# A new order for the same instructions: S and A blocks of several batches side by side on TensorE

## Chip, cores and metric

The kernel runs on one core of one Trainium2 chip. The time is the device time of one launch in microseconds (us); the median of several runs counts, and one more execution was taken by the hardware profiler.

## What is computed

The input x has 128 batches of 128 tokens (rows) by 512 features. adj is a 128 by 128 matrix, about one eighth of it not zero. Two layers follow each other, each with a residual and a normalization. Cut to what matters:

```
# layer 0: a product with adj, its maximum over the 512 columns, relu
C   = einsum('od,bdn->bon', adj, x) + b          # A is the same without b, so only
out = max over the last axis of relu(A_j + (C - A)_i)   # a row maximum of adj @ x is needed
x   = layernorm(x + out)

# layer 1: masked attention with 8 heads of 64, then a projection
q, k, v = split(x @ w_qkv)                       # 512 -> 3 x 512
attn = softmax(where(adj == 0, -inf, q @ k.T / 8))
o    = (attn @ v) @ w_proj + b_proj
x    = layernorm(x + o + layernorm(o) * gamma + beta)
```

## The kernel before

The 128 batches are worked in 32 groups of four. Within a group g, the batches b = 4g + i carry the index i = 0 to 3. All five queues (TensorE, VectorE, ScalarE, GpSimd and SP, which issues nearly all DMAs) are in an order written out by hand: no engine picks its next instruction by itself.

**How the order is made.** A step is a small function, such as S(b) or rest(g, j). Each step has a place, a number in planned microseconds from the group's start. Group g's places are moved by g times PERIOD, all places of all groups are sorted, and the steps are emitted in that order. So a place has no effect on the chip but through the order that comes out of it:

```
u0 = g * PERIOD
...
b, u = g * G + i, u0 + u
...
plan.sort(key=lambda p: p[:2])
with tc.manual_schedule(engines={E.PE, E.Activation, E.DVE, E.Pool, E.SP}):
    for _, _, f, a in plan:
        f(*a)
```

There are tables for groups 0 and 1 (FIRST), for the last two (LAST), for all the others (STEADY), and one for the weights and constants (SETUP). TWO says which steps use a two-bank tile or GpSimd. Waits between engines follow from the emitted order: a step that touches a tile waits for the steps ahead of it, in that order, that touch the same tile.

**The steps on TensorE.** All results lie in PSUM, where there are four one-bank buffers (ps_1) and two two-bank buffers (ps_2).

- conv(b), line 486: adj times x of one batch, for layer 0. Two matmul instructions.
- dm(g, j) and dd(g, j), lines 670, 671 and 676: the dense products for q, k and v. Operands are split into a high part h, a low part l and a difference d, so that one product is eight matmuls (dm: h times h, l times l) and four more (dd: d times d), into two banks. j = 0 to 3 are v of the four batches; j = 4 to 11 are column blocks of q and k, each for all four batches at once. Columns j = 0, 4 and 6 take one ps_2 buffer for both banks; the others take two ps_1 buffers.
- S(b), line 716: the scores q times k of one batch, 16 matmul instructions with 64 rows of the array, into a ps_2 buffer.
- AV(b), line 802, called A below: attention times v, 16 matmul instructions with 64 columns of the array.
- po(b) and pod(b): the projection, in the same eight and four matmuls as dm and dd; of the four batches, i = 2 takes a ps_2 buffer.

**The steps around them.** load(b) brings x in; cmax reduces conv's result on VectorE; relu, rstdx, shiftx and others on GpSimd make row factors, norm0 on ScalarE applies them. xpl, xrow and xcross transpose x through DRAM: ScalarE splits each word into two planes, SP writes them out and reads them back with a transposing DMA. xmask and xsub (VectorE), xhigh (ScalarE, or GpSimd for i = 0) and xd (VectorE or GpSimd) make the h, l and d parts of x, in buffers x_forms that there are once, with a slice for each batch of a group. So xhigh(b) of one group may write its slice only when the dense products of the group before have read it. main (ScalarE) takes the first bank of a dense product out, rest (VectorE) adds the second.

After S come masked and rmax (VectorE), exps (ScalarE, 16 instructions), recip and wts (VectorE), then pln (ScalarE), row and cross (SP), the same way through DRAM: cross(b), line 780, delivers the transposed weights eT that A(b) reads. After A come omask and osub (VectorE), ohigh (ScalarE or GpSimd), od (VectorE or GpSimd), then po and pod, pmain and prest (VectorE, they free the banks), sq1, st1, n1a, n1b, sq2, st2, norm2 for the last normalizations, with n1a and n1b (lines 892 and 865) on VectorE, and reso, resx, resb (the residual) and the small row operations on GpSimd. out(b) stores the result.

Of the kernel before, what the change touches and what calls it, by code (L numbers as in the profile page):

```python
# [26 lines left out]
PERIOD = 54.43882  # L27
STEADY = {
    'load': [-90.979, -98.210, -86.366, -88.446],
    'conv': [-75.080, -64.352, -67.023, -70.602],  # L30
    'cmax': [-72.886, -63.292, -64.469, -65.979],
    'relu': [-62.380, None, -61.262],
    'bn': [-85.283, -78.072],
    'ba': [-76.773, -76.871],
    'rstdx': [-64.783],
    'shiftx': [-61.992],
    'add0': [None, None, -60.500, -55.763],
    'sq0': [None, None, -56.469, -54.924],
    'rstd0': [None, None, -54.874],
    'shift0': [None, None, -23.855],  # L40
    'norm0': [-59.794, -61.212, -52.725, -52.013],
    'xpl': [-58.956, -54.218, -49.889, -44.844],
    'xrow': [-57.883, -53.145, -48.816, -43.301],
    'xcross': [-54.573, -50.568, -46.622, -40.435],
    'xmask': [-47.658, -42.468, -38.679, -34.118],
    'xsub': [-43.076, -38.349, -34.726, -32.646],
    'xhigh': [-47.158, -38.788, -33.148, -33.668],
    'xd': [-37.151, -28.807, -25.122, -23.029],
    'dm': [3.754, 7.444, 16.569, 13.785, -22.455, -31.523, -27.895, -19.783, -26.082, -24.268, -29.709, -4.527],
    'dd': [9.258, 19.289, 20.196, 11.065, -13.491, -8.148, -10.819, -9.055, -17.969, -15.305, -11.726, -2.714],  # L50
    'main': [9.110, 14.458, 21.811, 16.171, -10.671, -29.055, -11.156, -17.770, -24.069, -22.256, -17.285, -2.515],
    'rest': [12.301, 26.117, 23.001, 18.511, -5.215, -4.627, -1.871, -7.670, -15.367, -8.258, -10.618, -1.282],
    'S': [0.000, 0.970, 6.474, 15.599],
    'masked': [1.171, 4.033, 8.388, 26.711],
    'rmax': [2.907, 10.127, 14.634, 29.080],
    'exps': [6.022, 11.370, 22.296, 32.668],
    'recip': [11.253, 17.788, 27.842, 35.882],
    'wts': [12.895, 20.651, 37.253, 41.757],
    'pln': [16.656, 25.869, 38.513, 45.479],
    'row': [20.902, 29.660, 40.435, 47.401],  # L60
    'cross': [24.543, 33.020, 43.404, 51.435],
    'AV': [37.376, 47.198, 53.539, 64.603],
    'omask': [39.660, 48.620, 56.741, 72.345],
    'osub': [40.380, 50.401, 60.612, 73.544],
    'ohigh': [44.959, 51.471, 59.941, 73.606],
    'od': [48.023, 56.076, 68.476, 77.554],
    'po': [48.098, 56.379, 66.410, 75.542],
    'pod': [52.632, 60.006, 72.821, 94.480],
    'pmain': [51.968, 62.227, 76.840, 84.645],
    'prest': [53.745, 63.958, 78.638, 95.588],  # L70
    'res': [39.182, 60.502, 66.017, 83.629],
    'resx': [49.373, 64.496, 76.714, 86.509],
    'resb': [50.221, 68.714, 78.821, 88.081],
    'reso': [57.343, 70.378, 81.767, 96.358],
    'sq1': [57.577, 74.126, 82.111, 96.308],
    'sm1': [59.687, 67.486, 83.015, 100.647],
    'st1': [58.591, 75.013, 87.275, 102.706],
    'n1a': [59.947, 79.246, 91.027, 101.796],
    'n1b': [61.551, 82.391, 92.834, 105.448],
    'sq2': [64.986, 90.195, 98.692, 112.722],  # L80
    'sm2': [65.262, 89.331, 93.678, 113.836],
    'st2': [65.873, 91.082, 99.579, 114.416],
    'norm2': [72.898, 97.014, 105.313, 123.821],
    'out': [73.732, 100.113, 108.144, 131.860],
# [3 lines left out]
        'load': [-339.216, -336.022, -299.318, -292.716],  # L88
        'conv': [-320.211, -319.706, -263.923, -261.033],
        'cmax': [-287.550, -269.059, -253.277, -242.604],  # L90
        'relu': [-265.160, -255.522, -248.695, -239.422],
        'bn': [-289.729, -282.267, -262.447, -251.751],
        'ba': [-286.976, -275.167, -254.963, -248.112],
        'rstdx': [-273.222, -264.798, -251.699, -242.168],
        'shiftx': [-255.673, -255.423, -248.481, -238.547],
        'norm0': [-247.810, -241.423, -241.293, -231.100],
        'tx': [-239.998, -240.970, -235.970, -229.175],
        'copy': [-231.539, -232.867],
        'pv': [-186.452, -231.512],
        'keep': [-144.699, -223.445],  # L100
        'xmask': [-227.206, -233.390, -231.343, -223.813],
        'xsub': [-226.502, -230.254, -230.249, -179.216],
        'xhigh': [-210.161, -227.313, -226.698, -211.953],
        'xd': [-159.790, -216.301, -207.483, -146.722],
        'dm': [None, None, 14.000, 16.573, -19.708, -43.109, -33.492, -6.250, -23.281, -14.646, -35.590, -6.060],
        'dd': [None, None, 21.026, 20.229, -8.181, 0.474, -26.083, -12.473, -20.232, -14.110, -31.477, -1.951],
        'main': [None, None, 19.638, 24.293, -7.213, -26.572, -17.941, -3.776, -17.267, -10.053, -30.978, -2.703],
        'rest': [None, None, 21.313, 28.301, -4.316, 2.523, -15.800, 0.777, -7.778, -4.529, -14.235, 1.449],
        'S': [3.939, 4.174, 12.958, 20.307],
        'masked': [7.850, 9.636, 14.415, 22.403],  # L110
        'rmax': [8.329, 12.699, 21.343, 22.643],
        'exps': [13.089, 15.014, 24.976, 29.418],
        'recip': [16.256, 21.430, 34.750, 34.644],
        'wts': [20.131, 32.286, 38.995, 35.803],
        'pln': [22.222, 35.478, 41.768, 50.996],
        'row': [25.064, 45.158, 49.252, 57.729],
        'cross': [30.795, 46.513, 49.735, 59.800],
        'AV': [37.520, 47.772, 52.279, 66.968],
        'omask': [39.391, 49.259, 54.469, 70.965],
        'osub': [40.545, 53.566, 61.562, 72.912],  # L120
        'ohigh': [41.247, 52.725, 63.738, 71.968],
        'od': [50.703, 55.119, 66.836, 79.701],
        'po': [48.210, 53.595, 72.824, 76.960],
        'pod': [53.374, 57.260, 74.590, 81.809],
        'pmain': [51.767, 58.323, 83.163, 78.361],
        'prest': [54.212, 62.992, 84.049, 83.271],
        'res': [-6.851, 71.276, 49.227, 88.351],
        'resx': [22.755, 76.004, 61.128, 89.325],
        'resb': [32.496, 77.502, 65.105, 93.272],
        'reso': [55.887, 77.786, 86.372, 95.300],  # L130
        'sq1': [57.019, 72.242, 87.119, 86.554],
        'sm1': [57.798, 71.222, 86.212, 89.323],
        'st1': [67.763, 73.225, 87.146, 93.420],
        'n1a': [59.485, 81.416, 88.540, 103.102],
        'n1b': [69.341, 86.827, 89.211, 103.699],
        'sq2': [71.896, 89.208, 97.526, 112.672],
        'sm2': [75.269, 87.809, 90.158, 110.923],
        'st2': [75.788, 90.664, 99.514, 118.898],
        'norm2': [80.561, 97.480, 99.819, 134.926],
        'out': [82.775, 109.802, 103.140, 135.391],  # L140
    },
    {
        'load': [-144.852, -133.466, -152.643, -139.868],
        'conv': [-135.661, -121.160, -124.230, -125.568],
        'cmax': [-114.732, -91.366, -100.617, -106.235],
        'relu': [-83.301, None, -88.339],
        'bn': [-123.347, -101.036],
        'ba': [-122.535, -99.486],
        'rstdx': [-86.661],
        'shiftx': [-83.240],  # L150
        'add0': [None, None, -65.496, -86.773],
        'sq0': [None, None, -61.309, -81.741],
        'rstd0': [None, None, -59.490],
        'shift0': [None, None, 5.293],
        'norm0': [-74.823, -65.297, -57.477, -48.421],
        'xpl': [-69.704, -59.513, -56.889, -44.324],
        'xrow': [-60.039, -58.141, -47.326, -41.960],
        'xcross': [-60.034, -44.291, -41.474, -40.784],
        'xmask': [-51.323, -42.090, -40.930, -39.239],
        'xsub': [-44.906, -41.006, -36.993, -36.881],  # L160
        'xhigh': [-38.422, -39.691, -36.673, -37.554],
# [5 lines left out]
        'S': [-1.994, -0.002, -0.960, 21.339],  # L167
        'masked': [-0.617, 5.427, 2.141, 24.207],
        'rmax': [1.990, 8.305, 12.703, 26.036],
        'exps': [5.200, 16.787, 23.670, 28.218],  # L170
        'recip': [8.307, 19.928, 31.918, 29.464],
        'wts': [16.401, 28.492, 33.827, 37.853],
        'pln': [18.886, 28.689, 39.281, 43.942],
# [834 lines left out]
```

## Time and profile before

| What | Value |
|---|---|
| median of three runs | 1896.47 us (1894.26 to 1897.58) |
| the profiled execution | 1887.61 us, its span 1885.8 us |
| busy: TensorE, VectorE, ScalarE, GpSimd | 98%, 85%, 82%, 74% of the span |
| granted TensorE clock | 0.997 of full speed |
| DMA | 302.92 MB, mean 161 GB/s |
| issue to landing, median: cross, xcross, load | 4.3, 3.3, 3.0 us |
| first S at | 49.0 us |
| first S of the last group at | 1816.9 us |

The span runs from the first to the last instruction of the core; the execution's time lies around it. Busy time counts the profiled durations of instructions. For TensorE these overlap from one matmul to the next, so a step is better read as the difference of two starts. In profile lines, PE is TensorE, PEld its weight loads, DVE VectorE, ACT ScalarE and POOL GpSimd. "x16" at the end is the number of merged instructions, and in square brackets stands idle time ahead of a line and what ended it.

### The profile page before, as it was taken

The numbers are of one execution on the slowest core, as the hardware profiler recorded it, in microseconds if no ns is written. First come the engines' busy times: TensorE is split into PE (matmuls) and PEld (weight loads), VectorE is DVE, ScalarE is ACT, GpSimd is POOL, SyncE is SP. The second block draws the span as 40 slices with busy tenths as digits, with TensorE's granted clock in tenths as the row PEclk, the third lists the DMA queues.
The fourth block names the chain that finished last, engine by engine and source line by source line (L and its number), as shares of the span: only waits on it lengthen the run. The fifth ranks groups of instructions, "written<-read, shape, count | busy, mean of one in ns | idle before, by whom it ended". The sixth has DMA issues, their size and how long they took to land. (4 is left out here: it accounts for less than half of the span.)

```text
span 1885.8 us, 32740 instructions
## 1 busy us (share of the span) xinstructions
PE 1842.2 (98%) x10541; PEld 1417.9 (75%) x10541; DVE 1597.0 (85%) x2584; ACT 1542.4 (82%) x3927; POOL 1387.2 (74%) x1935
## 2 busy tenths in 40 slices
PE   8999999999999999999999999999999999999995
PEld 5677777777777777777777777777777777777774
DVE  7989888889888889888898888898888988888887
ACT  6977888888888888888888788888888888888775
POOL 4266787787777787777787777877777877777768
PEclk9999999999999999999999999999999999999998
DMA  5666566566565665665665656656566656666451
GB/s 149 158 159 169 162 169 164 166 161 176 154 173 160 161 184 163 156 164 166 160 186 147 164 163 166 178 162 160 160 168 167 180 147 169 168 163 171 141 139 51
DMA packets 486140, 302.92 MB, mean 161 GB/s; under 512 B 399440, under 2 KB 403664, under 8 KB 485968
## 3 DMA queue, kind: packets, MB, share of 16 engines
q1 hardware_dynamic: 485104, 299.70, 58.8%
q8 instruction: 84, 1.38, 0.3%
q10 hardware_dynamic: 864, 1.12, 0.2%
q14 instruction: 88, 0.72, 0.1%
HBM read 72.16 MB, written 131.07 MB: 108 GB/s over the span
## 5 line engine op out<-in xcount | busy, mean ns | idle before, releaser
L755 ACT ACTIVATE e<-e,nmax 128x128 f32<-128x128 f32 x1016 | 392.4, 390 | 0.0
L862 POOL TENSOR_TENSOR xb<-xb,o 128x512 f32<-128x512 f32 x125 | 199.5, 1596 | 77.1 <-DVE o L865 74.7
L770 ACT COPY planes<-e 128x2048 uint16<-128x2048 uint16 x124 | 234.8, 1893 | 20.6 <-DVE e L764 18.7
L876 POOL TENSOR_SCALAR sum<-sum 128x1 f32<-128x1 f32 (+1 forms) x287 | 99.1, 345 | 207.1 <-ACT square L871 193.2
L871 ACT ACTIVATE square<-o,sum 128x512 bf16<-128x512 f32 x256 | 183.4, 716 | 75.1 <-DVE o L865 74.2
L877 POOL TENSOR_TENSOR sum<-sum,mhalf 128x1 f32<-128x1 f32 (+1 forms) x287 | 212.8, 742 | 23.9
L755 ACT ACTIVATION_READ_ACCUMULATOR e<-e,nmax 128x1 f32 x1016 | 192.8, 190 | 0.0
L730 DVE SCALAR_TENSOR_TENSOR e<-psc,mask 128x1024 f32<-128x1024 f32 x127 | 154.3, 1216 | 42.5 <-PE psc L716 42.2
L858 POOL TENSOR_TENSOR xb<-xb,beta_sb 128x512 f32<-128x512 f32 x128 | 180.4, 1409 | 2.8
L764 DVE TENSOR_TENSOR e<-e,sums 128x1024 f32<-128x1024 f32 x128 | 159.5, 1246 | 0.0
L738 DVE TENSOR_REDUCE nmax<-e 128x8 f32<-128x1024 f32 x127 | 153.4, 1208 | 0.2
L607 POOL TENSOR_TENSOR x_d<-x_h,x_l 128x512 fp32r<-128x512 f32 x97 | 141.1, 1456 | 11.3 <-DVE x_l L613 10.2
L802 PEld LDWEIGHTS pav<-eT,v 128*64 128x64 f32 x2048 | 109.2, 136 | 49.1 <-issue 22.8
L716 PEld LDWEIGHTS psc<-qkT 64*128 64x128 f32 x2048 | 121.9, 187 | 31.1 <-issue 17.0
L802 PE MATMUL pav<-eT,v 128*64 128x128 f32 x2048 | 140.1, 279 | 3.2 <-DVE v L699 2.6
L716 PE MATMUL psc<-qkT 64*128 64x128 f32 x2048 | 140.7, 282 | 1.8 <-DVE qkT L699 1.4
L575 ACT COPY xplanes<-xt 128x1024 uint16<-128x1024 uint16 x124 | 128.7, 1038 | 15.8 <-DMA rowsx<-xplanes 14.6
L761 DVE RECIPROCAL sums<-sums 128x8 f32<-128x8 f32 x128 | 24.6, 192 | 133.1 <-ACT e L755 133.1
L486 PE MATMUL pa<-xt,adjT 128*128 128x512 f32 x256 | 134.7, 613 | 0.4 <-DVE adjT L415 0.4
L558 ACT ACTIVATE xt<-xt,sum 128x512 f32<-128x512 f32 x128 | 101.1, 810 | 40.4 <-POOL sum L552 20.4
L855 POOL TENSOR_SCALAR xb<-xb,sum 128x512 f32<-128x512 f32 x128 | 100.7, 787 | 34.5 <-DMA xb<-in_x_dram 33.2
L865 DVE SCALAR_TENSOR_TENSOR o<-o,sum,xb 128x512 f32<-128x512 f32 x128 | 125.3, 979 | 0.6
(4665 smaller groups left out, 5689.3 us busy)
## 6 DMA issues: line engine op xcount, KB each, us to landing
rows<-planes SPq DMA_DIRECT2D x124, 512.0 KB, 3.3
xt<-in_x_dram SPq DMA_DIRECT2D x128, 256.0 KB, 3.0
xb<-in_x_dram SPq DMA_DIRECT2D x128, 256.0 KB, 2.9
out_dram<-o SPq DMA_DIRECT2D x128, 256.0 KB, 3.0
rowsx<-xplanes SPq DMA_DIRECT2D x124, 256.0 KB, 2.8
wraw<-in_L_gnn_w_qkv_dram SPq DMA_DIRECT2D x8, 256.0 KB, 2.9
xT<-rowsx SPq DMA_TRANSPOSE x124, 3.3
eT<-rows SPq DMA_TRANSPOSE x124, 4.3
```

The source lines that it names most:

```text
L607: engine.tensor_tensor(d, h.bitcast(FP), l.bitcast(FP), op=ALU.subtract)
L716: nc.tensor.matmul(psc[:, s, hp, :], qkT[hs, hp, i, :], qkT[hs, KC + hp, i, :], start=not with_mask, stop=not with_mask or hp == HP - 1,)
L730: nc.vector.scalar_tensor_tensor(es[b], pscs.pop(b).rearrange("p s a m -> p (s a) m"), scale, mask_b, op0=ALU.mult, op1=ALU.add,)
L738: nc.vector.tensor_reduce(nmaxs[b], es[b], AX.X, ALU.max, negate=True)
L755: nc.scalar.activation(es[b][:, j, :], src[:, j, :], AF.Exp, bias=nmax[:, j : j + 1], scale=by, accum_out=sums[b][:, j : j + 1],)
L764: nc.vector.tensor_tensor(es[b], es[b], sums.pop(b)[:, :, None].to_broadcast([P, H, P]), op=ALU.mult,)
L770: nc.scalar.copy(pl, es.pop(b).rearrange("p h m -> p (h m)").bitcast(U16).rearrange("p (m s) -> p s m", s=2),)
L802: nc.tensor.matmul(pavs[b][s * HD : (s + 1) * HD, hp, :], v[:, h * HD : (h + 1) * HD], eT[:, s * HP + hp, :], start=True, stop=True,)
L858: nc.gpsimd.tensor_tensor(xbs[b], xbs[b], beta_sb, op=ALU.add)
L862: engine.tensor_tensor(xbs[b], xbs[b], os[b], op=ALU.add)
L871: nc.scalar.activation(square, src, AF.Square, bias=s[:, 0:1], scale=-float(D), accum_out=s[:, 1:2],)
L877: nc.gpsimd.tensor_tensor(s, s, mhalf[:, :n], op=ALU.pow)
```

## The change

No function is changed, and no instruction is added or removed; TWO is as it was. Changed are the numbers: PERIOD and all places in STEADY, FIRST, LAST and SETUP. The lines of STEADY that the text below speaks of (column i or j from left to right):

```diff
-PERIOD = 54.43882
+PERIOD = 55.65721
...
-    'xrow': [-57.883, -53.145, -48.816, -43.301],
-    'xsub': [-43.076, -38.349, -34.726, -32.646],
...
-    'dm': [3.754, 7.444, 16.569, 13.785, -22.455, -31.523, -27.895, -19.783, -26.082, -24.268, -29.709, -4.527],
-    'dd': [9.258, 19.289, 20.196, 11.065, -13.491, -8.148, -10.819, -9.055, -17.969, -15.305, -11.726, -2.714],
-    'main': [9.110, 14.458, 21.811, 16.171, -10.671, -29.055, -11.156, -17.770, -24.069, -22.256, -17.285, -2.515],
...
-    'S': [0.000, 0.970, 6.474, 15.599],
-    'cross': [24.543, 33.020, 43.404, 51.435],
-    'AV': [37.376, 47.198, 53.539, 64.603],
-    'ohigh': [44.959, 51.471, 59.941, 73.606],
-    'po': [48.098, 56.379, 66.410, 75.542],
-    'pod': [52.632, 60.006, 72.821, 94.480],
-    'prest': [53.745, 63.958, 78.638, 95.588],
...
+    'xrow': [-64.641, -56.635, -53.368, -45.398],
+    'xsub': [-48.801, -42.437, -37.819, -35.400],
...
+    'dm': [4.837, 11.201, 6.655, 16.122, -27.595, -10.169, -22.140, -32.141, -33.960, -23.959, -25.777, -30.323],
+    'dd': [9.383, 10.292, 20.788, 27.152, -12.896, -6.532, -8.350, -5.623, -4.714, -16.490, -7.441, -11.987],
+    'main': [7.711, 13.218, 9.668, 20.862, -11.380, -7.877, -11.865, -20.987, -31.942, -21.472, -23.760, -26.046],
...
+    'S': [0.000, 0.997, 13.110, 14.107],
+    'cross': [24.197, 29.995, 47.113, 59.806],
+    'AV': [37.158, 54.685, 53.762, 70.756],
+    'ohigh': [46.552, 56.528, 63.853, 84.748],
+    'po': [51.853, 58.675, 73.718, 96.599],
+    'pod': [57.646, 64.130, 75.536, 100.236],
+    'prest': [61.894, 65.455, 82.210, 102.843],
```

A place below zero is brought into a period by adding PERIOD: after, dd(g, 4) stands at -12.896 + 55.657 = 42.761 of the period ahead of its group. Sorted, TensorE's order over one period is as follows. A digit is i or j; a prime is the group before, a plus the group after; conv is that of the group after next.

```
before: S0 S1 po1' dm0 pod1' S2 dm1 dd0 A3' dd3 po2' dm3 S3 dm2 pod2' dd1 dd2 po3'
        dm5+ dm10+ dm6+ dm8+ dm9+ dm4+ conv0 dm7+ dd8+ A0 conv3 dd9+ pod3' dd4+
        conv2 dd10+ dd6+ conv1 dd7+ dd5+ A1 po0 dm11+ dd11+ pod0 A2
after:  S0 S1 pod0' po1' dm0 dm2 pod1' dd0 dd1 dm1 S2 S3 A3' dm3 po2' pod2' dd2
        dm8+ dm7+ dm11+ dd3 dm4+ dm10+ dm9+ dm6+ conv1 conv0 A0 conv3 dd9+ conv2
        po3' dd4+ dd11+ pod3' dm5+ dd6+ dd10+ dd5+ dd7+ dd8+ po0 A2 A1
```

Over the whole kernel, S and A blocks stand in 194 runs without another step between them before, and in 99 after. SP's order changes too: cross(2) stands ahead of xrow of the next group's first batch before, and behind it after.

In the table of the last group, the copy xhigh(124), which writes batch 124's slice of the high half of x, stands at -50.804 of that group, just behind dm(30, 0), at 4.851 of the group before (4.851 - 55.657 = -50.806), which reads that slice.

## The prediction

> **What bounds the kernel now.** I read the busy line of the page first, then the clock of the core, then TensorE's timeline of one middle group, then the waits in front of its products. The page and the windows view give this (in the window: length, then each engine's busy time):
>
> ```profile
> span 1885.8 us, 32740 instructions
> PE 1842.2 (98%) x10541; PEld 1417.9 (75%) x10541; DVE 1597.0 (85%) x2584; ACT 1542.4 (82%) x3927; POOL 1387.2 (74%) x1935
> 153.10:1763.90 1610.80, 1600.87 (x9194) 1238.04 (x9192) 1368.32 (x2214) 1342.84 (x3418) 1223.05 (x1681) 1.00 0.61 165
> ```
>
> TensorE is at 98%, at full clock, and the other engines have some 8 us of room in each group: VectorE 1368.32 / 28 = 48.9 us of a period of 57.5. So the middle is bound by TensorE's order and by what it does between products. The period comes from the timeline, where two S blocks start (cut by the window) 28 groups apart:
>
> ```profile
> 153.07 0.49 PE L716 MATMUL psc<-qkT 64*128 64x128 f32 x4
> ...
> 1763.93 0.49 PE L716 MATMUL psc<-qkT 64*128 64x128 f32 x4
> ```
>
> (1763.93 - 153.07) / 28 = 57.53 us a group. But 98% busy is no floor: a matmul's duration here contains pipelining, so I read steps from start to start. An S block alone, then the run A S S, then an A block alone, in the timeline of group 15 (columns: start, duration, instruction):
>
> ```profile
> 917.07 0.39 PE L670 MATMUL pm_(15, 3)_9858<-w_h,x_h 128*128 128x512 f32 x1
> 917.30 0.39 PE L671 MATMUL pm_(15, 3)_9858<-w_l,x_l 128*128 128x512 f32 x1
> 917.62 1.16 PE L716 MATMUL psc<-qkT 64*128 64x128 f32 x16
> 918.71 0.50 PE L670 MATMUL pm_(15, 2)_9892<-w_h,x_h 128*128 128x512 f32 x1
> 919.05 0.39 PE L671 MATMUL pm_(15, 2)_9892<-w_l,x_l 128*128 128x512 f32 x1
> ...
> 898.18 1.07 PE L676 MATMUL pd_('o', 56)_9651<-p_d,od 128*128 128x512 f32 x4
> 899.18 1.09 PE L802 MATMUL pav<-eT,v 128*64 128x128 f32 x16
> 900.20 2.06 PE L716 MATMUL psc<-qkT 64*128 64x128 f32 x32
> 902.19 0.50 PE L670 MATMUL pm_('o', 57)_9703<-p_h,oh 128*128 128x512 f32 x1
> 902.52 0.39 PE L671 MATMUL pm_('o', 57)_9703<-p_l,ol 128*128 128x512 f32 x1
> ...
> 949.50 1.07 PE L676 MATMUL pd_(16, 5)_10196<-x_d,w_d 128*128 128x512 f32 x4
> 950.50 1.09 PE L802 MATMUL pav<-eT,v 128*64 128x128 f32 x16
> 951.52 0.50 PE L670 MATMUL pm_('o', 60)_10221<-p_h,oh 128*128 128x512 f32 x1
> 951.86 0.40 PE L671 MATMUL pm_('o', 60)_10221<-p_l,ol 128*128 128x512 f32 x1
> ```
>
> A dense matmul steps by 0.23 us. The last one before S takes 0.32, the block 1.09, the first one after 0.34. Two S in a row take 1.99, so one more S in a run costs 1.99 - 1.09 = 0.90. Beyond 0.90, the lone S costs 0.09 + 0.19 + 0.11 = **0.39 us**. The lone A, with 0.90 taken for it too: 0.09 + 0.12 + 0.11 = **0.32**. The run A S S: 0.09 + 0.12 + 0.19 + 0.10 = **0.50** for three blocks.
>
> Second, waits that come back. The same timeline, and the totals in the answer for line 676 over this window (us, times):
>
> ```profile
> 910.65 1.21 PE L676 MATMUL pp_(15, 0)_9719<-w_d,x_d 128*128 128x512 f32 x4 [0.50 <-ACT v L695]
> ...
> 946.68 1.20 PE L676 MATMUL pp_(16, 6)_10005<-x_d,w_d 128*128 128x512 f32 x4 [0.19 <-ACT qkT L695]
> ...
>   ACT v L695: 5.0, 8
>   ACT qkT L695: 4.8, 25
> ```
>
> dd of columns 0 and 6 shares its two-bank tile with dm, and where main (ScalarE's read of bank one) stands ahead of dd in the order, dd waits for it. In the table of before, main(6) stands at 43.28 and dd(6) at 43.62, main(0) at 9.11 and dd(0) at 9.26: room for nothing, as main takes 0.6. Where dd stands ahead of main (column 4) there is no wait.
>
> **What the skill says.** *TensorEngine Tiling (Array Packing)*, Key Properties: "Changing tiling mode (not just tile) drains the TensorE". S uses half the rows, A half the columns, the rest the whole array, so A S S is three changes and a lone block two. The trace agrees: 0.50 / 3, 0.39 / 2, 0.32 / 2, all 0.16 to 0.20 us. *TensorE: Matmul & The Clock Gate*, Architectural detail: ScalarE and VectorE are strict FIFOs, and TensorE only pulls weight loads ahead. The stall at 910.65 agrees: everything behind dd(0) waits too. *SBUF — State Buffer* (shared port pair): a VectorE instruction with two SBUF inputs blocks against a GpSimd one that reads SBUF. The trace fits: n1b (line 865 with xb) goes from 0.74 us to 1.33 within a group.
>
> **The change, part by part.** No instruction is added or removed.
>
> *Runs of S and A.* A group of before has A2'S0S1, S2, A3', S3, A0, A1 (a prime: of the group before): 0.50 + 2 x 0.39 + 3 x 0.32 = 2.24 us, with 3 + 5 x 2 = 13 changes of mode, 0.172 each. After: A2'A1'S0S1, S2S3A3', A0: 3 + 3 + 2 = 8 changes, 1.38 us. Saved: 0.86. Block by block it is 0.50 + 0.51 + 0.32 = 1.33, saving 0.91. I take **0.9**. No row shows A behind A or A behind S. If each cost 0.12 more, 0.67 is saved; if A between two convs is cheaper than a lone one, up to 1.1. Over the 31 groups with such runs: **-28 us** (-21 to -34).
>
> *The order of main and dd.* After, main(0) is at 7.71 and dd(0) at 9.38, main(6) at 43.79 and dd(6) at 47.31: 1.1 and 2.9 us of room past main's 0.6. dd(4), at 42.76, stays ahead of main(4), 44.28. Both waits go. dd(6) comes 0.36 us late (1.69 from the dd ahead of it at 944.99 to 946.68, where a dd behind a conv usually takes 1.33), 25 times: 9 us. dd(0) lies between 5.0 us of TensorE idle and, as in group 15, 0.65 for each of 8 to 14 groups: 7. Together **-16 us** (-10 to -20).
>
> *What is late next.* In before, all other engines were placed to a period of 54.44 while TensorE took 57.53: 3.1 us of cushion in each group. After, they are placed to 55.66 against some 56.3, and most of it goes. Subtracting measured durations from the new places, the smallest margins ahead of TensorE are: po(1') behind ohigh(1') on GpSimd (0.87 + 1.83 against 3.02: 0.3 us); dd(9+) behind xd(3+) on VectorE (0.5); pod(2') behind od(2') (0.75); dm(8+) behind xsub(3+) (0.8); dm(4+) behind prest(2') (0.9). Before, margins of 0.4 to 0.7 (S0 behind rest(11), pod(3') behind rest(8)) left no regular wait. Unknown until run: below by 0, above by about 1.2 us a group, all five missed by 0.25. I take 0.25 us x 28 = **+7 us** (0 to +34). A gain under this head is excluded: it only adds waits.
>
> *The copy of a half of x.* xhigh(124) stands 0.002 behind dm(30,0), which reads that slice, where in before it stood 2.7 behind. It is one GpSimd instruction of 1.83 us, once. If GpSimd comes to it early it waits for that product, and reso(116), sm1(116) and st1(117) queue behind it, and n1a and n1b on VectorE behind those. The first dm of group 31, which needs the copy, is 17 us of places off. I take nothing: GpSimd's idle share of 26% covers it; without that cover it costs 2 to 4 us, once.
>
> *Loads, transposes and other engines' orders.* SP issues the same DMAs. load to conv keeps 9 us of places or more; row and cross are priced in the rival. Head and tail: TensorE idles 7.8 of the first 49 us, and GpSimd is busy 57.3 of the last 69. The same work in a new order; I take 0, with 6 us either way.
>
> Sum: -28 - 16 + 7 = **-37 us**. The profiled execution took 1887.61 us around its span of 1885.8, so 1850.6; the median of the runs is 1896.47, 8.9 us more, and the same saving gives **1860 us**. A group should take 57.53 - 0.9 - 0.57 + 0.25 = 56.3 us.
>
> **Rivals.**
> *Mostly eaten by VectorE (0.22).* Between places 9 and 32 the new VectorE order has hardly a gap. It gives xsub 0.61 us and n1b 0.68, where the groups show means of 0.92 and 0.98. Three and two of them stand ahead of prest(2'): 1.5 us late against margins of 0.8 and 0.9, so 0.6 us of wait at dm(8+) and dm(4+), and 0.3 at po(1') behind GpSimd. -28 - 16 + 25 = -19: 1877 us. For it: VectorE at 87% of 56 us. Against: it idles 4 us at place 32 and starts afresh.
> *Slower (0.14): the late transpose.* cross(2) moves from 43.40 to 47.11, since in SP's order it now stands behind xrow(4+), which waits for xpl on ScalarE and, through norm0 and shiftx, for GpSimd. A2 stays at 53.76: 6.65 us instead of 10.14, of which the transfer takes 4.3 (median to landing; 6.8 at most). Margin 2.35. Behind A2 stand A1, S0 and S1, so a wait there delays the next softmax too. From 2.35 + 1.32 = 3.7 us late on, the whole gain is lost; at 4.4 it costs 0.7 us x 28 = 20: 1916 us. For it: GpSimd's small operations stretch from 0.55 to 1.43. Against: before, the same cross was issued 1.9 us behind its place when TensorE itself was 2.5 behind.
> *It doesn't do what it says (0.04).* A run still pays for each block: -16 + 7: 1887 us.
>
> **How the numbers follow.** My forecast has 0.60, alone from 1844 to 1874. A measurement can tell about 0.2%, 4 us, from no change. Faster: 0.60 + 0.19 + 0.03 = 0.82; same 0.03; slower 0.15. The range reaches over the VectorE rival to 1892 and down to 1842, where all bounds of the gain meet no new wait; mostly the slow case is outside.
>
> **What would show it.** Right: S0 to S0 near 56.3 us; four-block and three-block runs with about 0.50 us around each; no "ACT v L695" or "ACT qkT L695" ahead of dd(0) and dd(6). Wrong: a wait ahead of A2 with a late eT (the slow rival), waits ahead of dm(4+) or dm(8+) that end with VectorE, a step of over 1.0 us for A behind A, or a head or tail that moves by over 6 us.

## The result and the profile after

| | before | after |
|---|---|---|
| median of four runs | 1895.61 us (1894.26 to 1897.58) | 1844.81 us (1843.79 to 1847.88) |
| ratio, with its 95% interval | | 0.9734 [0.9717, 0.9751] |
| first profiled execution (span) | 1887.61 (1885.8) | 1847.88 (1845.9) |
| second profiled execution (span) | 1893.17 (1891.4) | 1842.63 (1840.6) |

The change saves 50.8 us. The first two profiled executions differ by only 39.7 us: that of before was the fastest run of its kernel, that of after the slowest of four. The second pair, taken later on one chip, lies near the medians and differs by 50.8 us of span. Single lines in this section are from the first profile of after; the accounts in the last sections use the second pair. A third profile of after was taken with the runs on the last tables.

The busy line of the page of after, and the windows view from the first S of group 2 to that of group 30 (length, then busy time of TensorE, its weight loads, VectorE, ScalarE, GpSimd):

```profile
span 1845.9 us, 32707 instructions
PE 1807.2 (98%) x10541; PEld 1428.1 (77%) x10541; DVE 1549.0 (84%) x2584; ACT 1541.5 (84%) x3927; POOL 1310.9 (71%) x1935
```

```profile
146.89:1719.41 1572.52, 1564.86 (x9186) 1245.50 (x9184) 1323.42 (x2212) 1340.30 (x3416) 1144.11 (x1681) 1.00 0.64 169
```

TensorE is at 98% as before, with the same 10541 instructions, and yet the same work takes 40 us less, and its busy time itself fell by 35 us: it was no floor. VectorE's busy time fell too, by 48 us, though it does the same 2584 instructions. (The page's total is 33 lower, 32707 against 32740, but the counts of all engines shown are the same; the difference lies in instructions that the page doesn't count as work, such as waits.) The two starts that give the period, in TensorE's timeline:

```profile
146.89 0.49 PE L716 MATMUL psc<-qkT 64*128 64x128 f32 x4
...
1719.41 0.49 PE L716 MATMUL psc<-qkT 64*128 64x128 f32 x4
```

(1719.41 - 146.89) / 28 = 56.16 us a group; 56.3 was forecast. The mean hides a better number: 20 of the 28 groups take 55.58 us to within 0.01. Such a group is called calm here: it has no wait that varies from group to group. In before a calm group took 57.19. The three kinds of run, in the timeline of group 15 (start, duration, instruction):

```profile
873.18 0.39 PE L671 MATMUL pm_('o', 56)_9624<-p_l,ol 128*128 128x512 f32 x1
873.50 1.97 PE L802 MATMUL pav<-eT,v 128*64 128x128 f32 x32
875.40 2.06 PE L716 MATMUL psc<-qkT 64*128 64x128 f32 x32
877.38 1.20 PE L676 MATMUL pd_('o', 56)_9700<-p_d,od 128*128 128x512 f32 x4
878.41 0.39 PE L670 MATMUL pm_('o', 57)_9712<-p_h,oh 128*128 128x512 f32 x1
...
888.17 0.39 PE L671 MATMUL pm_(15, 1)_9807<-w_l,x_l 128*128 128x512 f32 x1
888.49 2.06 PE L716 MATMUL psc<-qkT 64*128 64x128 f32 x32
890.48 1.09 PE L802 MATMUL pav<-eT,v 128*64 128x128 f32 x16
891.50 0.50 PE L670 MATMUL pm_(15, 3)_9877<-w_h,x_h 128*128 128x512 f32 x1
891.84 0.39 PE L671 MATMUL pm_(15, 3)_9877<-w_l,x_l 128*128 128x512 f32 x1
...
910.68 1.88 PE L486 MATMUL pa<-xt,adjT 128*128 128x512 f32 x4
912.49 1.09 PE L802 MATMUL pav<-eT,v 128*64 128x128 f32 x16
913.51 1.13 PE L486 MATMUL pa<-xt,adjT 128*128 128x512 f32 x2
914.08 1.50 PE L676 MATMUL pd_(16, 9)_10106<-x_d,w_d 128*128 128x512 f32 x4
```

Two A in one merged line, then two S. From 873.18 to 878.41 pass 5.23 us; five dense steps of 0.228 and four blocks of 0.90 make 4.74, so the whole run costs 0.49 beyond its work. S S A takes 888.17 to 891.84 = 3.67; less two dense steps and 2.70 it costs 0.51. The A between convs costs about 0.32: 0.09 ahead of it (the conv instruction just before steps by 0.52 instead of 0.43), 0.12 on the block (1.02 instead of 0.90), 0.11 on the conv behind it (0.56 instead of 0.45). What dd still waits for, TensorE's own waits in the answer for line 676 over this window (us, times):

```profile
  DVE o L865: 3.2, 1
  DVE qkT L699: 0.8, 1
  ACT v L695: 0.6, 1
  POOL sum L876: 0.5, 1
  POOL x_d L607: 0.2, 1
```

"ACT qkT L695", 25 times before, is gone; "ACT v L695" is left once, in group 2. The one large entry is an incident in group 28. In VectorE's and TensorE's timelines:

```profile
1609.48 0.69 DVE L534 BATCH_NORM_STATS2 bnst<-xt 128x6 f32<-128x512 f32 x1 [4.05 <-DMA xt<-in_x_dram]
```

```profile
1610.92 2.04 PE L676 MATMUL pd_('o', 109)_17866<-p_d,od 128*128 128x512 f32 x4 [3.18 <-DVE o L865]
```

VectorE waits 4.05 us for the load of batch 120, and TensorE behind it for a bank. This group took 63.31 us. In the last tables bn(120) stands 2.3 us of places behind its load. The wait is not the whole loss: the four matmuls behind it last 2.04 us, where four of the kind last 1.07 elsewhere. In the windows view TensorE's granted clock (third number from the end) is 0.50 here:

```profile
1611.00:1616.60 5.60, 5.60 (x13) 4.35 (x14) 5.24 (x10) 1.63 (x4) 4.52 (x5) 0.50 0.52 140
```

Dense steps take 0.43 us instead of 0.23 until 1616.6, which costs another 2.7 us.

### The profile page after: what moved, and what is told of

Read it like the earlier page. It is cut to its first block, busy times and chain, and to the rows that moved or that the text cites. A ratio compares the mean times of both kernels' runs of the same rounds, so it can differ in the third digit from the quotient of the medians.

```text
span 1845.9 us, 32707 instructions
## 1 busy us (share of the span) xinstructions
PE 1807.2 (98%) x10541; PEld 1428.1 (77%) x10541; DVE 1549.0 (84%) x2584; ACT 1541.5 (84%) x3927; POOL 1310.9 (71%) x1935
## 3 DMA queue, kind: packets, MB, share of 16 engines
q8 instruction: 84, 1.38, 0.3%
## 5 line engine op out<-in xcount | busy, mean ns | idle before, releaser
L877 POOL TENSOR_TENSOR sum<-sum,mhalf 128x1 f32<-128x1 f32 (+1 forms) x287 | 194.4, 678 | 23.9
L862 POOL TENSOR_TENSOR xb<-xb,o 128x512 f32<-128x512 f32 x125 | 173.2, 1385 | 37.0 <-DVE o L865 34.5
L764 DVE TENSOR_TENSOR e<-e,sums 128x1024 f32<-128x1024 f32 x128 | 175.6, 1373 | 0.1
L858 POOL TENSOR_TENSOR xb<-xb,beta_sb 128x512 f32<-128x512 f32 x128 | 167.2, 1307 | 4.9
L876 POOL TENSOR_SCALAR sum<-sum 128x1 f32<-128x1 f32 (+1 forms) x287 | 122.5, 427 | 57.3 <-ACT square L871 37.8
L497 DVE TENSOR_REDUCE rm<-pa 128x1 f32<-128x512 f32 x128 | 87.9, 688 | 68.0 <-PE pa L486 66.4
L716 PE MATMUL psc<-qkT 64*128 64x128 f32 x2048 | 132.3, 279 | 0.6 <-DVE v L699 0.4
L607 POOL TENSOR_TENSOR x_d<-x_h,x_l 128x512 fp32r<-128x512 f32 x97 | 127.6, 1318 | 6.2 <-DVE x_l L613 6.1
L892 DVE SCALAR_TENSOR_TENSOR o<-o,sum,gamma_sb 128x512 f32<-128x512 f32 x128 | 99.5, 778 | 32.3 <-POOL xb L862 24.6
L880 POOL TENSOR_SCALAR sum<-sum 128x1 f32<-128x1 f32 x256 | 98.1, 384 | 22.2 <-DVE o L865 18.2
```

Of the source, the lines that this page charges most:

```text
L716: nc.tensor.matmul(psc[:, s, hp, :], qkT[hs, hp, i, :], qkT[hs, KC + hp, i, :], start=not with_mask, stop=not with_mask or hp == HP - 1,)
L764: nc.vector.tensor_tensor(es[b], es[b], sums.pop(b)[:, :, None].to_broadcast([P, H, P]), op=ALU.mult,)
L858: nc.gpsimd.tensor_tensor(xbs[b], xbs[b], beta_sb, op=ALU.add)
L862: engine.tensor_tensor(xbs[b], xbs[b], os[b], op=ALU.add)
L877: nc.gpsimd.tensor_tensor(s, s, mhalf[:, :n], op=ALU.pow)
```

## The experiments

The theory: the gain is (1) fewer changes of array mode and (2) main behind dd, and what is left over is new waits. Rivals: VectorE eats part of it; the late transpose decides; a run still pays for each block. A place is the only thing that is edited, so an edit acts through the order alone.

### Main behind dd, in the kernel before

```diff
-    'main': [9.110, 14.458, 21.811, 16.171, -10.671, -29.055, -11.156, ...
+    'main': [9.262, 14.458, 21.811, 16.171, -10.671, -29.055, -10.814, ...
```

> The kernel before with the places of main(g, 0) and main(g, 6) moved behind dd of the same columns in the steady groups; no engine's own order changes. Theory (the two regular waits of TensorE come from the order of these steps alone): both waits go, 0.36 us in 25 groups and some 0.65 us in 8 to 14: -16 us (-10 to -20), ratio 0.9916. Rival (the wait only hides another one behind it, or main, now later, holds up ScalarE): 0 to -4 us.

Measured: 1880.84 us against 1895.04, ratio 0.9918 [0.9903, 0.9933]: -15.5 us by the ratio, -14.2 between the medians. The calm group falls from 57.19 to 56.70 us. TensorE's waits in the answer for line 676, and who waits for it:

```profile
  DVE qkT L699: 0.4, 1
...
  ACT qkT L695: 38.9, 28
```

The wait did not vanish, it changed sides: ScalarE's main now waits for dd, where it costs nothing in a calm group. Of the 0.49 us in a calm group, 0.35 is the lateness of dd(6). Another 0.11, in 25 groups, is dd(6)'s own first step, 0.34 us behind the wait and 0.23 without it, which I had not counted. Groups 2 to 27 together are 19 us shorter than in the second profile of before. In this one execution groups 28 and 29, where the last tables begin, became long instead (58.99 and 65.67 us, 8 more than before): TensorE waits 1.8 and 2.7 us in dm(30, 10), and dense steps behind that take 0.43 us. The other runs of this kernel have no profile, so whether they share this is open.

### A3 next to S3, in the kernel before

```diff
-    'AV': [37.376, 47.198, 53.539, 64.603],
+    'AV': [37.376, 47.198, 53.539, 70.024],
```

> The kernel before with A(3) of the group before moved from behind dm(1), dd(0) to directly in front of S(3) in the steady groups. Theory (a change of the array's mode costs 0.17 to 0.21 us wherever it stands): one change fewer a group, 28 x 0.19 = -5 us, ratio 0.9972. Rival (each S or A block pays for itself, in a run or not): 0.

Measured: 1889.3 us, ratio 0.9966 [0.9954, 0.9978], -6.4 us. The calm group falls from 57.19 to 56.97: one change of mode less, 0.22 us. The interval excludes the rival's 0.

### The runs taken apart again, in the kernel after

```diff
-    'S': [0.000, 0.997, 13.110, 14.107],
-    'AV': [37.158, 54.685, 53.762, 70.756],
+    'S': [0.000, 0.997, 13.110, 19.870],
+    'AV': [37.158, 51.840, 53.762, 73.607],
```

> The kernel after with its runs taken apart again in the steady groups: A(1) ahead of po(0), A(3) behind dm(3), S(3) behind po(2); 13 changes of mode a group as before the change, instead of 8; all other engines as in after. Theory: 0.94 to 1.10 us more a group, +26 to +31 us on after, so some 0.988 of before. Rival (the gain lies in the new order of the other engines and the runs are worth little): within 6 us of after, 0.973 of before.

Measured: 1870.25 us, ratio to before 0.9868 [0.9854, 0.9883], 25.4 us more than after. In TensorE's timeline the blocks stand alone:

```profile
888.03 1.09 PE L802 MATMUL pav<-eT,v 128*64 128x128 f32 x16
889.05 2.06 PE L716 MATMUL psc<-qkT 64*128 64x128 f32 x32
...
902.15 1.16 PE L716 MATMUL psc<-qkT 64*128 64x128 f32 x16
...
905.28 1.09 PE L802 MATMUL pav<-eT,v 128*64 128x128 f32 x16
...
908.34 1.16 PE L716 MATMUL psc<-qkT 64*128 64x128 f32 x16
```

A1 alone (not shown) adds two changes of mode, S2, A3 and S3 apart add three. The calm group takes 56.60 us, 1.02 more, in 20 of 28 groups alike: 0.20 us for each change. This refutes the rival that a run pays for each block, and the one that the gain lies in the new order of the other engines. All other engines had one more microsecond in each group, the period stayed at 56.60 flat, and TensorE's timeline has no wait over 0.1 us in these groups: it is TensorE's own time and no wait.

### The transpose later still, in the kernel after

```diff
-    'cross': [24.197, 29.995, 47.113, 59.806],
+    'cross': [24.197, 29.995, 50.900, 59.806],
```

> The kernel after with cross(2) moved back in SP's order from place 47.11 to 50.90, behind xcross of the next group's first batch and behind one store. Theory (margin of A(2) behind the transpose 53.76 - 47.11 - 4.3 = 2.35 us): 3.8 us later is 1.4 to 1.6 us too late, each group waits so long in front of A(2): +40 to +45 us on after, about 0.996 of before. Rival (the wait is taken up by slack elsewhere, or TensorE's later places carry it): under +10 us.

Measured: 1916.28 us, ratio to before 1.0112 [1.0094, 1.013], 71.5 us more than after. SP's and TensorE's timelines, and TensorE's waits:

```profile
958.43 2.01 SPq L780 DMA_TRANSPOSE eT<-rows  x1
```

```profile
963.05 1.97 PE L802 MATMUL pav<-eT,v 128*64 128x128 f32 x32 [1.79 <-DMA eT<-rows]
964.95 2.06 PE L716 MATMUL psc<-qkT 64*128 64x128 f32 x32
```

```profile
PE pav L802 <- DMA eT<-rows: 59.8, 28, 5.0
```

This cross(2) is issued at 958.43, and 4.6 us later A2 can start. The slow rival's mechanism is real, and its point lies where it was put: in after, line 802 waits for no DMA at all, and 3.8 us of places later each of 28 groups waits, 2.1 us on average. In the 15 groups without other trouble the wait is 1.6 to 2.1 us and the group longer by just that, close to the 1.4 to 1.6 forecast: 28 times that would be 50 us. The mean group is 58.66 us, 2.6 more than in the second profile of after. The rest, some 23 us, lies in the other groups. There the wait is longer, up to 5.0 us, and in seven of them (2, 7, 16, 23, 24, 28 and 29) the granted clock falls to 0.50 for 3.4 or 6.8 us. Group 23, in TensorE's timeline and in the windows view:

```profile
1429.51 3.68 PE L802 MATMUL pav<-eT,v 128*64 128x128 f32 x32 [3.83 <-DMA eT<-rows]
1433.12 3.18 PE L716 MATMUL psc<-qkT 64*128 64x128 f32 x32
```

```profile
1429.50:1434.00 4.50, 4.49 (x40) 4.17 (x42) 0.78 (x2) 1.04 (x1) 0.00 (x1) 0.50 0.65 257
```

The same two lines last 1.97 and 2.06 us in the group shown above. I had counted only the lateness of A2 in a calm group, and a long wait costs more than its length. The clock does not fall behind each such wait: behind 2.61 us in group 3 it stays.

### Mending what is left: the copy, bn and main in the last tables

These three and the kernel after ran on one chip.

> The kernel after, unchanged, so that the next three are compared with it on the same chip: 1845 us, 50 us under the kernel before.

Measured: 1844.21 us (1843.71 to 1846.57), ratio to before 0.975 [0.9737, 0.9764].

The copy xhigh(124), in the last group's table:

```diff
-        'xhigh': [-50.804, -39.714, -37.872, -37.053],
+        'xhigh': [-48.100, -39.714, -37.872, -37.053],
```

> The kernel after with the copy xhigh(124) set 2.7 us of places further behind dm(30,0), as it stood in the table before (-50.804 becomes -48.100 in the last group's table). In the profile of the kernel after this copy waits 0.74 us for the product dm(30,0) that reads its slice. Theory that the copy costs nothing, because its reader dm(31) comes 17 us of places later and GpSimd has room: within 2 us of the kernel after. Rival, the copy's wait holds up reso, sm1 and st1 behind it and through them VectorE: 2 to 4 us under the kernel after.

Measured: 1845.52 us, ratio to before 0.9755 [0.9742, 0.9769]: nothing, as forecast. In GpSimd's timeline of after the copy does wait for the product that reads its slice, and that is the whole of it:

```profile
1726.10 1.50 POOL L601 TENSOR_SCALAR x_h<-xh 128x512 fp32r<-128x512 f32 x1 [0.74 <-PE pp_(30, 0)_19056 L670]
```

bn further behind its load, in the table of the last but one group:

```diff
-        'bn': [-105.550, -89.567],
-        'ba': [-85.955, -88.221],
+        'bn': [-92.000, -84.500],
+        'ba': [-85.955, -83.000],
```

> The kernel after with bn(120) and bn(121) moved behind their loads by 15.8 and 7.2 us of places instead of 2.3 and 2.1 (-105.550 becomes -92.000, -89.567 becomes -84.500, and ba(121), which reads bn's result, -88.221 becomes -83.000, in the table of the last but one group). Theory: group 28's 63.3 us against 55.6 in the regular groups, and part of group 29's 57.0, come from VectorE waiting 4.05 us for load(120) in bn(120), with masked, osub and prest queued behind it. Then group 28 falls to about 56 us and the time by 6 to 9 us, to 1837 to 1840. Rival: group 28 is long because the table of the last groups fits badly as a whole (other places where main stands ahead of dd, another order): less than 2 us.

Measured: 1842.73 us (1841.89 to 1844.36), ratio 0.9741 [0.9728, 0.9755]: 1.5 us less, and the intervals overlap. My theory took one execution for the rule. In three more profiles that leave bn where it was, bn(120) waits 1.6 to 2.7 us instead of 4.05, and group 28 takes 59.4 to 60.8 us, not 63.3; with bn later it takes 58.9. The incident is worth at most 1 to 2 us. Even then TensorE waits 1.6 us ahead of pod(109) and 0.5 us ahead of dm(29, 10) in this group; what makes it longer than 55.6 was not taken apart further.

Main behind dd in the last two tables, on top of it:

```diff
-        'main': [11.351, ...
+        'main': [14.125, ...
...
-        'main': [16.401, 30.773, 43.694, 37.058, -19.124, ...
+        'main': [17.530, 30.773, 47.610, 37.058, -18.815, ...
```

> As the run with the later bn(120) and bn(121), and main set behind dd where the last two tables still have it ahead in a two-bank tile: main(31,0) 16.401 becomes 17.530, main(31,4) -19.124 becomes -18.815, main(31,2), a one-bank column for comparison, 43.694 becomes 47.610, main(30,0) 11.351 becomes 14.125. In the profile of the kernel after, dd(31,0) waits 2.0 us, dd(31,4) 1.1 us and dd(30,0) 0.5 to 0.7 us behind main. Theory that such a wait on TensorE is lost time wherever TensorE is the bound: 2 to 4 us under the run with the later bn alone, 1834 to 1837. Rival: at the end TensorE waits for VectorE's and ScalarE's chain of the last group anyway, so that the wait only moves: within 1 us.

Measured: 1842.25 us (1840.61 to 1844.52), ratio 0.9738 [0.9725, 0.9752]: 0.5 us less than with bn alone. The waits of dd(31,0), 2.0 us, and of dd(31,4), 1.1 us, are gone from TensorE's waits, and nothing is won that the measurement can tell. In this profile other waits stand in their place, 0.7 us ahead of dm(31, 10) and 0.9 ahead of pod(119), and group 30 takes 55.71 us instead of 55.04. That speaks for the rival: removing a wait there only moves it. A gain of 2 us, the lower end of the theory, is not excluded by so few runs.

### The wait behind the output DMA

The regular groups hold one more wait. In every fifth group or so (5, 8, 13, 18, 23), TensorE loses 0.3 to 1.2 us, mostly ahead of dm(4+), dm(10+) or dm(9+). Followed back in the third profile of after (of the section above, up to 1640 us), it starts on VectorE, whose pmain (line 839) needs the buffer o that out(3) of the group before last is still reading (us, times, longest):

```profile
DVE o L839 <- DMA out_dram<-o: 7.3, 7, 2.0
```

In this profile the DMA lands 5.1 to 5.5 us after its issue in these five groups and, from group 4 on, 3.9 to 4.3 in the others. In SP's order it stands behind res(2), which waits for a buffer. The edit puts it ahead:

```diff
-    'out': [97.230, 106.460, 109.286, 132.611],
+    'out': [97.230, 106.460, 109.286, 131.000],
```

The measure on the same chip:

> The kernel after, unchanged, as the measure for the next two on the same chip: 1844 us.

Measured: 1844.0 us, ratio to before 0.9734 [0.972, 0.9747].

> The kernel after with one step of SP earlier: out(3) of the group before last goes ahead of res(2), which waits 1.3 us for n1a to free xb (STEADY, out[3] 132.611 becomes 131.000). Theory: the waits ahead of dm(4+), dm(10+) and dm(9+) in every fifth group begin with VectorE's pmain(2'), which waits for the DMA of out(3'') to free the buffer o: it lands after 5.2 to 5.5 us in these groups and after 4.0 to 4.3 in the others. Issued some 1.5 us earlier it is always there in time: the 7 waits of pmain on this DMA (7.3 us in all) go, groups 5, 8, 13, 18 and 23 fall from 56.2 to 56.7 to 55.6, group 28 by about 1 us, 4 to 7 us under the kernel after. Rival, VectorE itself is late there, and the wait for the DMA is only where it shows: within 2 us.

Measured: 1856.74 us, ratio 0.9797 [0.9784, 0.981]: 12.7 us slower. Half of the theory held: pmain's waits for this DMA fell from 7 to 1. But row(0), which feeds cross(0), now stands behind out(3). A group where it shows, in SP's timeline:

```profile
785.52 0.34 SPq L916 DMA_DIRECT2D out_dram<-o  x1
786.23 0.33 SPq L852 DMA_DIRECT2D xb<-in_x_dram  x1
786.61 0.44 SPq L776 DMA_DIRECT2D rows<-planes  x1
```

In ScalarE's and TensorE's:

```profile
793.49 1.90 ACT L770 COPY planes<-e 128x2048 uint16<-128x2048 uint16 x1 [3.40 <-DMA rows<-planes]
...
798.91 0.58 ACT L695 ACTIVATE qkT<-pm_(14, 11)_8727 128x512 f32<-128x512 f32 x1
```

```profile
799.54 0.50 PE L670 MATMUL pm_(14, 9)_8795<-x_h,w_h 128*128 128x512 f32 x1 [2.13 <-ACT qkT L695]
```

row(0) is issued at 786.61 and lands 6.8 us later. In most groups it now takes 4.2 to 4.6 us, where in the third profile of after it took 3.7 to 4.2, behind res(2) and ahead of out(3), and in groups 13 and 18 it takes 6.8 instead of 5.0 to 5.2; out(3) itself falls to 2.4 to 3.2 us. There is one buffer planes, so pln(1) waits 3.40 us; the exps and main(11+) queue behind it on ScalarE, and dm(9+) waits 2.13 us for the bank that main(11+) frees. In groups 18 and 28 the granted clock also falls to 0.50 for 3.4 us behind such a wait. ScalarE's waits for rows over the middle are 20.2 us with the order of after (second profile) and 34.6 with this one, and the median group rises from 55.58 to 55.80. My reading, which no run tests further: of the two transfers the later one bears the longer landing, and after's order gives it to the one with the cheaper follower.

> The earlier out(3) and the later bn(120) and bn(121) together: 1836 to 1840 us if both hold, group 28 at 57 to 58 us.

Measured: 1851.83 us, ratio 0.9773 [0.9759, 0.9786]: the loss again, since it holds the same edit. No kernel here beats after by more than the measurement can tell.

### A second profile of before

> The kernel before, unchanged, for a second profile: the first one was 8 us under the median of its runs. If that is scatter of the execution, some groups in the middle are longer here by 1 us or more; if the profile itself runs faster, this one lies as far below the median again.

Measured: 1893.17 us, 1.2 under the median of nine runs. Its mean middle group is 57.61 us against 57.53 in the first profile, and its first S comes at 50.9 instead of 49.0. The 8 us were scatter of one execution, partly in its first 50 us, and no property of a profiled run.

## Why the prediction was right, point by point

The forecast was -37 us, 1860; it became -50.8, 1844.81, near the lower end of the range. The mechanisms were as forecast; the sizes of the terms were not all. By the account below, 10 of the 13.8 us beyond the forecast lie in groups 2 to 29: 3.4 for the price of a change of mode, 6 for dd's waits, 2.8 at the convs, which the prediction did not hold, less 2 for more new waits. The other 4 lie at the two ends.

**Runs of S and A: -28 forecast; 1.02 us in a calm group and 25.4 us in all measured by taking them apart.** Counting changes of mode, 13 to 8, was right; the price of a change was the mis-sized term. I took 0.17 to 0.18 us; the calm groups of the two runs that add or take away changes give 0.20 and 0.22. Read again with unrounded starts, before's blocks cost 2.40 us a group instead of 2.24: up to seven dense steps behind each run are a little long, some 0.03 us together, which the first reading left out. After's cost 1.38, the upper end of the 1.33 to 1.38 expected. The difference, 1.02, is what the runs taken apart show too. Over 31 groups that is an estimate of 32 us; the edit itself, in 28 groups, cost 25.4, as its long groups exceeded the calm one by 9 us in all and those of after by 12.7. A behind A, the unknown that set the lower bound, adds nothing visible: A A S S costs as much as A S S. The reason for the upper bound, a cheaper A between convs, was not seen: A0 costs 0.32 in both.

**The convs, not in the forecast.** The kernel before with main behind dd has 13 changes and takes 56.70 us in a calm group; after with its runs taken apart has 13 as well and takes 56.60. Followed step by step, this 0.10 lies in the stretches with the four convs and A0, which cost 0.51 us beyond their work in the first and 0.41 in the second. In after two of the convs stand side by side. No run moved a conv alone.

**Main and dd: -16 forecast, -15.5 measured** by the edit alone. The agreement is partly luck. In a calm group it is 0.49 us and not 0.36, mostly since the first step behind the wait is longer by 0.11; dd(0) cost 8.4 us in the second profile of before, where I took 7. By this count it is some 22 us in the middle, of which the edit's profile shows 19 in groups 2 to 27. The edit alone gave 8 of them back in its two long groups at the end.

**What is late next: +7 forecast, some +9 measured, in other places.** The five margins were expected to fail a little in each group. None fails in a calm group. The tightest place on the VectorE side, dm(4+) behind prest(2'), is where the waits of every fifth group appear, but they begin at an output DMA that the list of margins did not hold. By the second pair of profiles, the groups of after lie 28 x (56.04 - 55.58) = 12.7 us above the calm one: 4 in the fifth groups, 3 in group 2, 6 in groups 28 and 29. Before, it was 28 x (57.61 - 57.19) = 11.9, of which 8.4 are dd(0)'s; 12.7 - 3.5 = 9.

**The sum for groups 2 to 29:** -28.6 (1.02 x 28) - 2.8 (0.10 x 28) - 13.7 (0.49 x 28) - 8.4 + 9.2 = -44.3, against a measured 28 x (57.61 - 56.04) = -44. This is an account and no second test: the first three terms are steps between the calm groups of four kernels, and the others come from the same two profiles. What is tested twice is the 1.02. Outside them: groups 0 and 1 gain 5.4 us, nearly all in group 1 (60.36 to 55.62). The prediction had there only the runs' 0.9 a group, and where the rest comes from was not taken apart. The first S is 2.7 us earlier, about the scatter of one kernel; group 30 and the tail together lose 1.5. That head and tail stay within 6 us holds for the time up to the first S and for the tail; with groups 0 and 1 the head gains 8.

**The base.** The saving was put on the median as it was on the profile, and that was right: the second profile of before shows that the first was a fast execution.

**The copy: 0 forecast, 0 measured.** It waits 0.74 us, covered as said.

**The rivals.** "Mostly eaten by VectorE" would have shown as VectorE waits in every group; they are in a few. "It doesn't do what it says" falls with the runs taken apart. The late transpose did not come in after, but the run with a later cross shows that it is there at once when the margin is used up. The rival's price, 2.05 us in each of 28 groups or 57 us, had the wait about right (2.1 on average) and was too small in all (71.5), as it did not hold what stands behind a long wait. That its 1916 was then measured for this run (1916.28) is chance: the gain it started from was larger too.

## What to carry to other kernels

Busy time that stays at 98% can still hide 3% in the gaps of start-to-start steps: count the changes of array mode and put blocks of one mode side by side, and blocks of two modes next to each other rather than each alone. Let an engine that has room wait for the bound one: where two steps share a buffer and only the order decides who waits, emit the bound engine's step first. (This paid in the steady groups; in the last tables it won nothing that could be told.) Look at the granted clock behind a wait of the bound engine: the wait can cost more than its length. Before a wait on a DMA is mended by an earlier issue, look up what stands behind the transfers that it passes.

## What the runs showed of the hardware beyond what was expected

- A change between whole array, half of the rows and half of the columns costs 0.20 to 0.22 us here (1.02 for five in one run, 0.22 for one in another), and two blocks of the same half in a row need none (A A S S costs 0.49 us beyond its work, A S S 0.50).
- With some waits of TensorE the granted clock fell to 0.50 for 3.4 or 6.8 us, from the wait's end or shortly before or after it: with 3.18 us in group 28 of after and 1.87 in its second profile, with 1.99 to 5.0 us in seven groups of the run with the later cross. With 2.61 us in group 3 of that run it did not. At 0.50 a dense step took 0.43 us instead of 0.23.
- The same DMA of 256 KB, out(3), at the same place of the order, lands after 3.9 to 4.5 us in most groups of the three profiles of after and after 4.7 to 5.5 in groups 5, 8, 13, 18, 23 and 28 (4.0 in group 5 of the second profile). row(0), 512 KB, which is issued next to it, is late in groups 5, 13, 18, 23 and 28 of the first and third profile as well (4.6 to 5.2 us instead of 3.7 to 4.2). What makes it so is open.
- VectorE's busy time over the same instructions fell from 1597.0 to 1549.0 us and GpSimd's from 1387.2 to 1310.9 with the new order, and the later profiles repeat it (1596.6 to 1550.1, 1390.6 to 1308.0). No run here took this apart.
